# The last key chunk by paired block products inside the product with V, and the token maximum split over two batches

## The chip, the cores and the metric

The kernel runs on one core of one Trainium2 chip. A core has TensorE (PE in the profile; PEld are its weight loads), VectorE (DVE), ScalarE (ACT), GpSimd (POOL) and SyncE (SP, which here only issues DMAs). Matmul results go to PSUM, which has eight banks of 512 f32 columns; POOL works on SBUF only in this kernel. The metric is the device time of one execution in microseconds (us), given as a median of several runs.

## The reference, cut to what matters

There are 16 batches, each with 100 rows of x (640 wide), 718 rows of encoder states and 4 tokens (both 384 wide). All arithmetic is f32. Heads are 8 of 80 columns.

```python
query = hidden_states @ Wq                       # 100 x 640
keyt = enc @ Wk                                  # 718 x 640
valt = enc @ Wv                                  # 718 x 640
hs = _mha(query, keyt, valt)                     # 8 heads over 718 keys
ca_q1 = jnp.einsum('btc,th->bch', ca, Wq_ca)     # from the 4 tokens
ca_q1 = ca_q1[:, indices, :]                     # 100 of 384 rows
ca_hs1 = _mha(ca_q1, residual, residual)         # softmax 1, over the rows of x
ca_q2 = ca_hs1 @ Wq
ca_hs2 = _mha(ca_q2, ca @ Wk_ca, ca @ Wv_ca)     # softmax 2, over the 4 tokens
out = (hs + ca_hs2) @ Wout + b_out + residual
```

## The kernel before

The loop runs over the batches b. In batch b PE makes the scores and the values of b and, ahead of time, the keys of b + 1. The order of instructions on every engine is that of the program text, since the loop runs under a manual schedule; each engine works through its own list in order, and waits on semaphores where a tile that it reads or overwrites is not ready.

Keys and values are products of three row thirds and three column chunks of the encoder states with the weights. Most are not made by the usual 18 block products for a 3 x 3 by 3 x 2 block matrix but by 15, from sums of blocks (`V_PLAN` and `K_PLAN`). The sums of encoder blocks are made on POOL (`enc_sums`, L506), those of weights once at the start (`weight_sums`, L528). In a plan, each entry names a chain (A to E), a product and a place. The products of one chain are added up in one PSUM bank. After each product the bank, as it stands, is read once and goes to that entry's place: copied by ACT if the place is new (L413), added by DVE if it has been written before (L411). So the next product of a chain has to wait until the bank has been read.

The 640 key columns are five chunks of 128. Chunks 0 to 3 go through `Keys` (L471), two chunks a product. The fifth goes through `last_keys` (L565): nine plain matmuls of 128 columns of weights (`wk4`) with 240 keys, 18 passes since an f32 matmul makes two, into a pair of banks, and two copies by ACT (L576) into `kT`.

In a batch from the second to the one before the last, PE does in this order: scores in three groups (`s_ps`, L620), `z_ps` (L808) of the second softmax path, `y_ps` (L746), the transposes of the batch before (`hst_ps`), 15 value products and 15 key products in turns (L440, L471), `last_keys`, the projection of earlier rows (`o_ps`, L951, in 11 batches in all), the queries of the next two batches (`q_ps`, L541, in odd batches), and the product with V (`a_ps`, L1317). That has two groups of four heads; each entry of a group is a pair of matmuls, one with 64 columns of weights and one with 36, in the two column halves of PE's array, 81 columns wide. Group 0 goes first over the keys of all four heads by tile, group 1 head by head. After a group DVE takes the reciprocal of the sums (L1329), multiplies (L1331) and adds `hs2`, the token part (L1338).

The first softmax of the token path is over `e1` (100 x 800). POOL makes it for batch b + 1 (`scores1`, L781, L788) during batch b. Its maximum is found by `Maximum`: DVE turns the tile (L672), reduces it (L674, L677, L684), spreads the maxima (by DVE, L699, or, with `scalar`, by ACT, L694) and turns them back (L702); `softmax1` then subtracts (L798) and `exponentials1` takes the exponential on ACT (L801). In batches from the second on, all this stands after `last_keys` and ahead of `a_ps`. The keys' maxima of the main softmax (`most`, L1156 and L1168; `st`, L1144 and L1152) go through the same engines.

PSUM is in three pools of two: `ps2` (pairs of banks: block chains A and B of the values, `last_keys`, `o_ps`, scores groups 0 and 2), `psk` and `ps1` (single banks: the other chains, queries, scores group 1, `a_ps`). `psum` takes from the last two in turn. The row third (1, 0) and (2, 2) of the encoder states have a single tile, `rest`, which SP loads for batch b + 2 behind the reads of `last_keys` and of `enc_sums`.

Of the kernel before, what the change touches and what calls it, by code (L numbers as in the profile page):

```python
# [8 lines left out]
F32 = mybir.dt.float32  # L9
# [9 lines left out]
P = 128  # L19
# [56 lines left out]
def load_packed(load, to, w):  # L76
# [37 lines left out]
    ("A", 0, (0, 1)),  # L114
    ("B", 14, (0, 0)),
    ("A", 5, (1, 1)),
]

K_PLAN = [V_PLAN[k] for k in (0, 1, 2, 3, 4, 6, 5, 7, 9, 11, 8, 12, 10, 13, 14)]
# [13 lines left out]
def kernel(  # L133
# [117 lines left out]
    def a_form(enc, f):  # L251
        return enc[0][:, A_AT[f]]
# [4 lines left out]

    wv_sb = const.tile([P, NF, H // 2], F32, name="wv_sb")
    wk_sb = const.tile([P, NF, 2, P], F32, name="wk_sb")
    wk4 = const.tile([P, CC, P], F32, name="wk4")  # L260
    wq_sb = const.tile([P, HC, H], F32, name="wq_sb")
    kT = const.tile([P, HC, 3, KT], F32, name="kT")
    wout_sb = const.tile([P, HC, H], F32, name="wout_sb")
# [100 lines left out]
    e1 = const.tile([P, ROWS], F32, name="e1")  # L364
    nc.gpsimd.memset(e1[96:, :], LOW)

    ys = []
    for j in range(2):
        y = const.tile([S, NH, HT + 1], F32, name=f"y_{j}")
        nc.gpsimd.memset(y[:, :, HT:], 1.0)  # L370
        ys.append(y)


    def first_values(i, enc, engines, halves=(0, 1), get=psum):
# [19 lines left out]
    class Blocks:  # L394


        def __init__(self, plan):
            self.opened, self.begun = {}, set()
            self.plan = iter(enumerate(plan))
            self.ends = {bank: k for k, (bank, _, _) in enumerate(plan)}  # L400
# [15 lines left out]
    class Values(Blocks):  # L416
# [17 lines left out]
        def product(self, at, f, first, last):  # L434
            for bank in "AB":
                if self.opened[bank] is at and bank in self.fresh:
                    first = True
                    self.fresh.discard(bank)
            for j in range(2):
                nc.tensor.matmul(  # L440
                    at[0][j][:KN, : H // 2],
                    a_form(self.enc, f)[:, j * KN : (j + 1) * KN],
                    wv_there.get(f, wv_sb[:, W_AT[f]]),
                    start=first,
                    stop=last,
                    skip_group_check=True,
                )
# [142 lines left out]
    def last_keys(b, enc):  # L590
        banks = pair(f"kT_ps_{b}")
        return chunk_keys(
            HC - 1,
            [banks[:, k] for k in range(2)],
            [wk4[:, c] for c in range(CC)],
            enc,
        )


    def scores(b, g, tiles):  # L600
# [124 lines left out]
    class Second:  # L725


        def __init__(self, b, xT, ca=None):
            self.b, self.xT = b, xT[:, b % 2]
            self.top = None  # L730

            self.ca = ca
            if ca is not None:
                return
            self.ca = small.tile([S, T, S], F32, tag="ca", name=f"ca_{b}", bufs=2)
            nc.sync.dma_start(
                out=self.ca, in_=cas[b].unsqueeze(0).to_broadcast([S, T, S])
            )
# [23 lines left out]
            return summed  # L762

        def copy(self):
            b, y_ps = self.b, self.y_ps
            self.y = ys[b % 2]
            nc.scalar.copy(
                self.y[:, :, :HT].rearrange("p (u h) k -> p u h k", u=2),
                y_ps[:S, HT : 11 * HT].rearrange("p (u h k) -> p u h k", u=2, h=5)[
                    :, :, :4, :  # L770
                ],
            )
# [19 lines left out]
        def softmax1(self, n=8):  # L792

            if not self.top:
                self.top = Maximum(e1, f"1_{self.b}")
            self.top.go(n)
            if self.top.over is not None:
                nc.vector.tensor_tensor(e1[:S], e1[:S], self.top.over[:S], ALU.subtract)  # L798

        def exponentials1(self):  # L800
# [255 lines left out]
    for c in range(HC):  # L1056
        w_ps = psum(f"w_ps_{c}")
        for cc in range(CC):
            nc.tensor.transpose(
                w_ps[:, cc * P : (cc + 1) * P], wkt_sb[:, c, cc * P : (cc + 1) * P], ident  # L1060
            )
        act(
            wk_sb[:, c % 2 : 6 : 2, c // 2] if c < HC - 1 else wk4,
            w_ps[:, : CC * P].rearrange("p (a n) -> p a n", a=CC),
        )

# [55 lines left out]
    for b in range(B):  # L1122
# [38 lines left out]
        if b == 0:  # L1161
            enc_sums(enc)
            now.load()
            now.softmax1()
        st.append(scores(b, 0, tiles))
        if b == 0:
            now.exponentials1()
        nc.vector.tensor_tensor(most[:KN], st[0][:, 0], st[0][:, 1], ALU.max)  # L1168
        st.append(scores(b, 1, tiles))
# [12 lines left out]
        if b == 0:  # L1182
            second.scores1()
            m_next = load_m(b + 2)
            kk.go(3)
            top.go(3)
            first_values(3, e_in, (act, act), get=bank)
            top.go(1)
            kk.go(2)
            now.scores2()  # L1190
            first_values(0, e_in, (act, act), (0,), bank)
            top.go()
            kk.go(3)
            first_values(0, e_in, (act, act), (1,), bank)
            now.softmax3()
            kk.go(2)
            subtract(0)
            exponential(0)
            kk.go(2)
            subtract(1)  # L1200
            kk.go(3)
            exponential(1)
            second_next, enc_next = loads()
            less = subtract(2)
            exponential(2)
            last_keys(b + 1, enc)
            enc_next = load_rest(b + 2, enc_next)
            keys(m_next)
            now.values2(less)
            enc_sums(enc_next)  # L1210
            second.softmax1(4)
        elif b + 1 < B:
            if b > 1:
                last.transpose()
            vv = Values(b, e_in)

            def both(n):
                vv.go(n)
                kk.go(n)

            second.scores1(seen)
            if b == 1:
                now.load()
            last.load()
            top.go(3)
            both(3)
            now.scores2()
            top.go(1)
            both(2)
            if b == 1:  # L1230
                nc.vector.tensor_tensor(last.hs[:S], last.hs[:S], last.hs2, ALU.add)
            top.go()
            both(2)
            if b == 1:
                last.transpose(get=psum1)
            both(1)
            now.softmax3()
            now.values2()
            vv.go(2)
            kk.go(1)  # L1240
            subtract(0)
            exponential(0)
            vv.go(1)
            subtract(1)
            vv.go(1)
            kk.go(2)
            exponential(1)
            vv.go(1)
            kk.go(2)
            both(1)  # L1250
            both(1)
            if b == 1:
                for f in list(wv_there):
                    nc.scalar.copy(wv_sb[:, W_AT[f]], wv_there.pop(f))
            second.load()
            if b == 1:
                nc.gpsimd.dma_start(out=bias, in_=bout[0].partition_broadcast(P))
            second_next, enc_next = loads()
            if b + 2 < B:
                m_next = load_m(b + 2)  # L1260
            subtract(2)
            exponential(2)
            last_keys(b + 1, enc)
            if b + 2 < B:
                enc_next = load_rest(b + 2, enc_next)
            second.softmax1()
            last.project()
        else:
            room = enc_tile("spare").rearrange("p f k -> p (f k)")
            spare.extend(room[:, i * H : (i + 1) * H] for i in range(2))  # L1270
            last.transpose()
            vv = Values(b, e_in)
            last.load()
            mine.load()
            top.go(3)
            vv.go(3)
            last.project_few(len(OC) - 2)
            now.scores2()
            top.go(1)
            vv.go(2)  # L1280
            top.go()
            vv.go(3)
            now.softmax3()
            now.values2()
            vv.go(2)
            subtract(0)
            exponential(0)
            vv.go(5)
            for i in (1, 2):
                subtract(i)  # L1290
                exponential(i)
            last.project()
# [3 lines left out]
        if b % 2 and b + 1 < B:  # L1296
            xT, tiles = xT_at[0], queries_tiles(p + 1)
            for n in range(HC):
                queries(p + 1, xT, tiles, n)
        if 0 < b < B - 1:  # L1300
            second.exponentials1()

        mine.hs = hs = hs_tile(f"hs_{b}")
        hs2 = now.hs2
        for g in range(2):
# [3 lines left out]
            order = [(h, i) for h in range(4 * g, 4 * g + 4) for i in range(len(KC))]  # L1309
            if g == 0:  # L1310
                order.sort(key=lambda at: at[1] // 2)
            for h, i in order:
                if b == B - 1 and h == NH - 1 and i == 0:

                    mine.transpose([(0, 2)])
                for lo, hi in QC:
                    nc.tensor.matmul(  # L1317
                        a_v[lo:hi, h % 4],
                        st[i // 2][: KEYS[i], i % 2, h * S + lo : h * S + hi],
                        block(i, h // 4)[: KEYS[i], h % 4],  # L1320
                        start=(i == 0 and h in (0, *range(4, NH))),
                        stop=(i == len(KC) - 1),
                        skip_group_check=True,
                    )
# [71 lines left out]
```

## Time and profile before

| what | value |
| --- | --- |
| runs | 943.58, 943.99, 944.01 us; median 943.99 |
| span of the profiled execution, first to last instruction | 942.4 us; the page gives no other time of that execution |
| PE busy | 934.5 us, 99% of the span |
| DVE, POOL, ACT busy | 674.0, 623.1, 364.7 us |
| granted TensorE clock | 1.000 |
| chain that ended last: PE share | 96% |
| of it, `a_ps`; `kT_ps` | 12%; 8% |

A line of groups gives the source line, engine, operation, output and inputs, shape and count; then, after the bar, busy us in total and mean ns of one, and then the idle time of the engine just before, with what ended it. A timeline line gives start (us), duration (us), and the same names; an idle time is in square brackets. A line of waits has the waiting instruction, what it waited for, and the total us, the number and the longest. Durations of PE matmuls overlap, since they are pipelined; the chain of work in order of time gives each piece the time until the next one.

### The profile page before, as it was taken

The numbers are of one execution on the slowest core, as the hardware profiler recorded it, in microseconds if no ns is written. First come the engines' busy times: TensorE is split into PE (matmuls) and PEld (weight loads), VectorE is DVE, ScalarE is ACT, GpSimd is POOL, SyncE is SP. The second block draws the span as 40 slices with busy tenths as digits, with TensorE's granted clock in tenths as the row PEclk, the third lists the DMA queues.
The fourth block names the chain that finished last, engine by engine and source line by source line (L and its number), as shares of the span: only waits on it lengthen the run. The fifth ranks groups of instructions, "written<-read, shape, count | busy, mean of one in ns | idle before, by whom it ended". The sixth has DMA issues, their size and how long they took to land.

```text
span 942.4 us, 25629 instructions
## 1 busy us (share of the span) xinstructions
PE 934.5 (99%) x11215; PEld 796.2 (84%) x11215; DVE 674.0 (72%) x1084; ACT 364.7 (39%) x605; POOL 623.1 (66%) x565
## 2 busy tenths in 40 slices
PE   9999999999999999999999999999999999999998
PEld 6998979888797888989789887987989888897866
DVE  3559794977929688595955959578693886949684
ACT  1244443524334244433424334244431534334241
POOL 5857976776738757495873948657694576748514
PEclk9999999999999999999999999999999999999999
DMA  8822024040310404003050130403113030210300
GB/s 264 296 60 87 3 70 128 1 130 3 94 60 1 117 2 135 5 11 122 1 151 3 37 82 1 139 1 95 38 40 113 1 112 7 59 53 1 95 8 29
DMA packets 45367, 62.48 MB, mean 66 GB/s; under 512 B 13448, under 2 KB 37320, under 8 KB 43656
## 3 DMA queue, kind: packets, MB, share of 16 engines
q1 hardware_dynamic: 41720, 42.97, 15.2%
q0 software_dynamic: 2512, 16.72, 6.1%
q8 instruction: 88, 1.44, 0.6%
q10 hardware_dynamic: 1024, 1.15, 0.4%
q14 instruction: 23, 0.19, 0.1%
HBM read 55.26 MB, written 5.57 MB: 65 GB/s over the span
## 4 chain that ended last, share of the span: by engine, by line
PE 96%; DVE 3%; issue 0%; DMA 0%; ACT 0%; POOL 0%; ACTq 0%; DVEq 0%
PE s_ps L620 12%; PE a_ps L1317 12%; PE v_psA L440 10%; PE v_psB L440 8%; PE kT_ps L565 8%; PE k_psA L471 7%; PE q_ps L541 7%; PE o_ps L951 7%; PE k_psB L471 6%; PE v_psC L440 3%; PE k_psC L471 3%; PE y_ps L746 2%; PE v_ps L381 2%; PE v_psD L440 2%; PE v_psE L440 2%; PE k_psE L471 1%
## 5 line engine op out<-in xcount | busy, mean ns | idle before, releaser
L781 POOL TENSOR_TENSOR e<-ca,g 100x800 f32<-100x800 f32 x64 | 99.8, 1570 | 145.2 <-DVE most L1156 125.0
L870 POOL TENSOR_TENSOR hs<-vb,p 100x640 f32<-100x640 f32 x64 | 105.6, 1659 | 45.9 <-DVE p L856 32.5
L877 POOL TENSOR_TENSOR hs<-hs,hs 100x640 f32<-100x640 f32 x48 | 113.9, 2373 | 3.8
L1317 PEld LDWEIGHTS a_ps<-vs,st 120*36 120x36 f32 (+3 forms) x3072 | 109.1, 125 | 5.6 <-issue 5.5
L1317 PE MATMUL a_ps<-vs,st 120*36 120x81 f32 (+3 forms) x3072 | 111.9, 233 | 0.0
L440 PE MATMUL v_psA<-wv_sb,enc 128*120 128x320 f32 x352 | 109.5, 434 | 0.0
L506 POOL TENSOR_TENSOR enc<-enc 128x240 f32<-128x240 f32 x135 | 98.1, 736 | 16.9 <-DMA enc<-in_enct 9.8
L1144 DVE TENSOR_TENSOR st<-st,over 120x1600 f32<-120x1600 f32 x48 | 107.6, 2243 | 0.0
L637 ACT COPY st<-s_ps 120x800 f32<-120x800 f32 x64 | 49.7, 829 | 135.6 <-PE s_ps L620 135.6
L620 PE MATMUL s_ps<-qp,kT 32*120 32x100 f32 x3072 | 97.4, 263 | 0.0
L620 PEld LDWEIGHTS s_ps<-qp,kT 32*120 32x120 f32 x3072 | 94.7, 179 | 1.6 <-issue 0.2
L788 POOL TENSOR_TENSOR e<-e,e 100x800 f32<-100x800 f32 x48 | 90.4, 1884 | 3.8
L440 PE MATMUL v_psB<-wv_sb,enc 128*120 128x320 f32 x296 | 91.9, 433 | 0.0
L471 PE MATMUL k_psA<-enc,wk_sb 128*128 128x240 f32 x360 | 87.6, 366 | 0.0
L1329 DVE RECIPROCAL rs<-a_ps 100x4 f32<-100x4 f32 x32 | 5.8, 182 | 111.0 <-PE a_ps L1317 111.0
L1156 DVE TENSOR_TENSOR most<-most,st 120x800 f32<-120x800 f32 x64 | 66.2, 1034 | 24.1 <-ACT st L631 23.0
L1152 ACT ACTIVATE st<-st 120x1600 f32<-120x1600 f32 x48 | 73.9, 1539 | 22.3 <-DVE st L1144 22.2
L471 PEld LDWEIGHTS k_psA<-enc,wk_sb 128*128 128x128 f32 x360 | 68.2, 190 | 16.8 <-DVE kT L411 0.2
L440 PEld LDWEIGHTS v_psA<-wv_sb,enc 128*120 128x120 f32 x352 | 63.2, 183 | 22.6 <-issue 0.5
L471 PE MATMUL k_psB<-enc,wk_sb 128*128 128x240 f32 x300 | 73.1, 366 | 0.3 <-DVE sm L853 0.3
L440 PEld LDWEIGHTS v_psB<-wv_sb,enc 128*120 128x120 f32 x296 | 54.0, 183 | 21.9 <-DVE vs L411 0.4
L541 PE MATMUL q_ps<-xT,wq_sb 128*128 128x200 f32 x400 | 69.1, 333 | 0.0
(146 smaller groups left out, 1732.8 us busy)
## 6 DMA issues: line engine op xcount, KB each, us to landing
vb<-va_d POOLq DMA_DIRECT2D x16, 1000.0 KB, 7.4
enc<-in_enct SPq DMA_DIRECT2D x30, 240.0 KB, 3.9
enc<-in_enct SPq DMA_DIRECT2D x15, 360.0 KB, 3.6
xT<-in_xt SPq DMA_DIRECT2D x8, 500.0 KB, 4.3
rest<-in_enct SPq DMA_DIRECT2D x31, 120.0 KB, 6.6
xn<-in_x SPq DMA_DIRECT2D x11, 320.0 KB, 5.7
out<-xn SPq DMA_DIRECT2D x11, 320.0 KB, 3.2
ca<-in_cas SPq DMA_DIRECT2D x16, 156.2 KB
```

What stands on the lines that cost most here:

```text
L440: nc.tensor.matmul(at[0][j][:KN, : H // 2], a_form(self.enc, f)[:, j * KN : (j + 1) * KN], wv_there.get(f, wv_sb[:, W_AT[f]]), start=first ...
L471: nc.tensor.matmul(at[:, i * KT : (i + 1) * KT], wk_sb[:, W_AT[f], i], a_form(self.enc, f), start=(first and i == 0), stop=last, skip_grou ...
L506: nc.gpsimd.tensor_tensor(out, left, right, op)
L541: nc.tensor.matmul(q_ps[:, : 2 * S].rearrange("p (j s) -> p j s", j=2), wq_sb[:, c, n * P : (n + 1) * P], xT[:, :, c, :], start=(c == 0), ...
L565: nc.tensor.matmul(bank[:, i * KT : (i + 1) * KT], weights[c], a_raw(enc, u, c), start=(i == 0 and c == 0), stop=(c == CC - 1), skip_group ...
L620: nc.tensor.matmul(s_ps[r][:n, 256 * a + lo : 256 * a + hi], kT[rows, c, u, j * KN : (j + 1) * KN], rhs, start=(a == 0 and c == 0), stop=( ...
L781: first = nc.gpsimd.tensor_tensor(to, self.ca[:, t, :].unsqueeze(1).to_broadcast([S, NH, S]), g[:, :, t].unsqueeze(2).to_broadcast([S, NH, ...
L788: nc.gpsimd.tensor_tensor(e, e, to, ALU.add)
L870: first = nc.gpsimd.tensor_tensor(to, vb[:S, t, :].rearrange("p (h d) -> p h d", h=NH), p2[:, :, t].unsqueeze(2).to_broadcast([S, NH, D]), ...
L877: nc.gpsimd.tensor_tensor(sums, sums, to, ALU.add)
L1144: return nc.vector.tensor_tensor(st[i], st[i], top.over[:KN].unsqueeze(1).to_broadcast([KN, 2, ROWS]), ALU.subtract,)
L1317: nc.tensor.matmul(a_v[lo:hi, h % 4], st[i // 2][: KEYS[i], i % 2, h * S + lo : h * S + hi], block(i, h // 4)[: KEYS[i], h % 4], start=(i ...
```

## The change

The fifth chunk of the keys of batches 2 to 15 is no longer made by `last_keys`. It is made by the same 15 block products, with `wk5` holding 64-column blocks of weights and their sums (the differences are made once, on POOL, in batch 1). `REST_PLAN` puts them in eight steps. Seven steps are two products of 64 columns of weights with 240 keys, one in each column half of PE's array, in two banks; one step is a single product, split in its keys over the halves. The steps stand inside the product with V: one after the first pair of each group of heads, and then every six pairs, four steps in each group. After a step its two partial sums are read from PSUM, by ACT where the place in `kT` is new and by DVE where it has been written. Chain A has six of the products, in steps 0, 2, 4, 5, 6 and 7. Banks A and B are from `psk`, D and C are a pair of `ps2`. The first two key sets (batches 0 and 1) still go through `last_keys`.

The maximum of `e1` for batches from 2 on is spread by ACT instead of DVE, and stops there ahead of the projection; the transpose back and the subtraction go to the start of the next batch, ahead of its scores, and the exponential behind the copies of its first scores. One `y` tile is left of two.

```diff
@@ -114,6 +114,17 @@
     ("A", 0, (0, 1)),
     ("B", 14, (0, 0)),
     ("A", 5, (1, 1)),
+]
+
+REST_PLAN = [
+    (("A", 7, (2, 1)), ("B", 13, (1, 0))),
+    (("D", 1, (2, 0)), ("C", 12, (0, 1))),
+    (("A", 3, (2, 0)), ("B", 8, (2, 0))),
+    (("E", 6, (1, 0)),),
+    (("A", 9, (1, 0)), ("C", 11, (2, 1))),
+    (("A", 2, (0, 0)), ("B", 10, (2, 1))),
+    (("A", 0, (0, 1)), ("B", 4, (0, 1))),
+    (("A", 5, (1, 1)), ("B", 14, (0, 0))),
 ]
 
 K_PLAN = [V_PLAN[k] for k in (0, 1, 2, 3, 4, 6, 5, 7, 9, 11, 8, 12, 10, 13, 14)]
@@ -257,7 +268,7 @@
 
     wv_sb = const.tile([P, NF, H // 2], F32, name="wv_sb")
     wk_sb = const.tile([P, NF, 2, P], F32, name="wk_sb")
-    wk4 = const.tile([P, CC, P], F32, name="wk4")
+    wk5 = const.tile([P, NF, P // 2], F32, name="wk5")
     wq_sb = const.tile([P, HC, H], F32, name="wq_sb")
     kT = const.tile([P, HC, 3, KT], F32, name="kT")
     wout_sb = const.tile([P, HC, H], F32, name="wout_sb")
@@ -364,11 +375,8 @@
     e1 = const.tile([P, ROWS], F32, name="e1")
     nc.gpsimd.memset(e1[96:, :], LOW)
 
-    ys = []
-    for j in range(2):
-        y = const.tile([S, NH, HT + 1], F32, name=f"y_{j}")
-        nc.gpsimd.memset(y[:, :, HT:], 1.0)
-        ys.append(y)
+    y_sb = const.tile([S, NH, HT + 1], F32, name="y_sb")
+    nc.gpsimd.memset(y_sb[:, :, HT:], 1.0)
 
 
     def first_values(i, enc, engines, halves=(0, 1), get=psum):
@@ -592,9 +600,69 @@
         return chunk_keys(
             HC - 1,
             [banks[:, k] for k in range(2)],
-            [wk4[:, c] for c in range(CC)],
+            [
+                wk5[:, 2 * c : 2 * c + 2].rearrange("p g n -> p (g n)")
+                for c in range(CC)
+            ],
             enc,
         )
+
+    class LastKeys:
+
+
+        def __init__(self, b, enc):
+            self.b, self.enc = b, enc
+            self.banks, self.begun = {}, set()
+            self.steps = iter(REST_PLAN)
+
+        def product(self, bank, half, f, lo, keys, n, first):
+            nc.tensor.matmul(
+                bank[64 * half : 64 * half + 64, lo : lo + n],
+                wk5[:, W_AT[f]],
+                a_form(self.enc, f)[:, keys : keys + n],
+                start=first,
+                stop=True,
+                skip_group_check=True,
+            )
+
+        def read(self, bank, half, to, lo, keys, n):
+            u, g = to
+            out = kT[64 * g : 64 * g + 64, HC - 1, u, keys : keys + n]
+            left = bank[64 * half : 64 * half + 64, lo : lo + n]
+            if to in self.begun:
+                nc.vector.tensor_tensor(out, left, out, ALU.add)
+            else:
+                nc.scalar.copy(out, left)
+
+        def open(self, chains):
+            name = f"k5_ps_{self.b}"
+            if chains == "AB":
+                self.banks |= {c: psumk(f"{name}_{c}") for c in "AB"}
+            elif chains == "DC":
+                both = pair(name)
+                self.banks |= {"D": both[:, 0], "C": both[:, 1]}
+
+        def go(self, n=1):
+            for _, step in zip(range(n), self.steps):
+                if len(step) == 1:
+                    ((_, f, to),) = step
+                    parts = [
+                        (self.banks[c], half, f, to, KT, half * KN, KN, False)
+                        for half, c in enumerate("DC")
+                    ]
+                else:
+                    first = step[0][0] not in self.banks
+                    if first:
+                        self.open("".join(c for c, _, _ in step))
+                    parts = [
+                        (self.banks[c], half, f, to, 0, 0, KT, first)
+                        for half, (c, f, to) in enumerate(step)
+                    ]
+                for bank, half, f, _, lo, keys, m, first in parts:
+                    self.product(bank, half, f, lo, keys, m, first)
+                for bank, half, _, to, lo, keys, m, _ in parts:
+                    self.read(bank, half, to, lo, keys, m)
+                self.begun |= {to for _, _, to in step}
 
 
     def scores(b, g, tiles):
@@ -727,7 +795,7 @@
 
         def __init__(self, b, xT, ca=None):
             self.b, self.xT = b, xT[:, b % 2]
-            self.top = None
+            self.top, self.less = None, False
 
             self.ca = ca
             if ca is not None:
@@ -762,8 +830,8 @@
             return summed
 
         def copy(self):
-            b, y_ps = self.b, self.y_ps
-            self.y = ys[b % 2]
+            y_ps = self.y_ps
+            self.y = y_sb
             nc.scalar.copy(
                 self.y[:, :, :HT].rearrange("p (u h) k -> p u h k", u=2),
                 y_ps[:S, HT : 11 * HT].rearrange("p (u h k) -> p u h k", u=2, h=5)[
@@ -792,9 +860,10 @@
         def softmax1(self, n=8):
 
             if not self.top:
-                self.top = Maximum(e1, f"1_{self.b}")
+                self.top = Maximum(e1, f"1_{self.b}", self.b > 1)
             self.top.go(n)
-            if self.top.over is not None:
+            if self.top.over is not None and not self.less:
+                self.less = True
                 nc.vector.tensor_tensor(e1[:S], e1[:S], self.top.over[:S], ALU.subtract)
 
         def exponentials1(self):
@@ -1060,7 +1129,9 @@
                 w_ps[:, cc * P : (cc + 1) * P], wkt_sb[:, c, cc * P : (cc + 1) * P], ident
             )
         act(
-            wk_sb[:, c % 2 : 6 : 2, c // 2] if c < HC - 1 else wk4,
+            wk_sb[:, c % 2 : 6 : 2, c // 2]
+            if c < HC - 1
+            else wk5[:, :6].rearrange("p (a g) n -> p a (g n)", a=CC),
             w_ps[:, : CC * P].rearrange("p (a n) -> p a n", a=CC),
         )
 
@@ -1161,9 +1232,9 @@
         if b == 0:
             enc_sums(enc)
             now.load()
-            now.softmax1()
+        now.softmax1()
         st.append(scores(b, 0, tiles))
-        if b == 0:
+        if b != 1:
             now.exponentials1()
         nc.vector.tensor_tensor(most[:KN], st[0][:, 0], st[0][:, 1], ALU.max)
         st.append(scores(b, 1, tiles))
@@ -1254,16 +1325,16 @@
                     nc.scalar.copy(wv_sb[:, W_AT[f]], wv_there.pop(f))
             second.load()
             if b == 1:
+                weight_sums(nc.gpsimd, wk5)
                 nc.gpsimd.dma_start(out=bias, in_=bout[0].partition_broadcast(P))
             second_next, enc_next = loads()
             if b + 2 < B:
                 m_next = load_m(b + 2)
             subtract(2)
             exponential(2)
-            last_keys(b + 1, enc)
             if b + 2 < B:
                 enc_next = load_rest(b + 2, enc_next)
-            second.softmax1()
+            second.softmax1(4)
             last.project()
         else:
             room = enc_tile("spare").rearrange("p f k -> p (f k)")
@@ -1297,8 +1368,7 @@
             xT, tiles = xT_at[0], queries_tiles(p + 1)
             for n in range(HC):
                 queries(p + 1, xT, tiles, n)
-        if 0 < b < B - 1:
-            second.exponentials1()
+        k5 = LastKeys(b + 1, enc) if 0 < b < B - 1 else None
 
         mine.hs = hs = hs_tile(f"hs_{b}")
         hs2 = now.hs2
@@ -1309,7 +1379,9 @@
             order = [(h, i) for h in range(4 * g, 4 * g + 4) for i in range(len(KC))]
             if g == 0:
                 order.sort(key=lambda at: at[1] // 2)
-            for h, i in order:
+            for at, (h, i) in enumerate(order):
+                if k5 and at % 6 == 1:
+                    k5.go()
                 if b == B - 1 and h == NH - 1 and i == 0:
 
                     mine.transpose([(0, 2)])
```

## The prediction

> **What bounds the kernel now.** I read the page's busy times first, then the chain of work that ended last, then the waits of TensorE.
>
> ```profile
> PE 934.5 (99%) x11215; PEld 796.2 (84%) x11215; DVE 674.0 (72%) x1084; ACT 364.7 (39%) x605; POOL 623.1 (66%) x565
> PE 96%; DVE 3%; issue 0%; DMA 0%; ACT 0%; POOL 0%; ACTq 0%; DVEq 0%
> ```
>
> TensorE (PE) is busy for 99% of the span at the full granted clock, and the chain is PE. The chain in order of time (start, us, what, passes; each f32 matmul makes two passes) shows two batches:
>
> ```profile
> 49.44 1.77 PE va_ps L1090 x12
> ...
> 365.52 3.65 PE kT_ps L565 x18
> 369.17 8.46 PE q_ps L541 x50
> 377.62 6.91 PE a_ps L1317 x191
> 384.53 7.28 PE s_ps L620 x240
> ...
> 422.39 3.65 PE kT_ps L565 x18
> 426.04 5.38 PE o_ps L951 x20
> 431.42 6.91 PE a_ps L1317 x191
> ```
>
> Each piece starts where the last one ended, so a batch has no slack: a us taken from PE is a us gained, and a us that PE waits is a us lost. The waits of PE confirm it; the longest, in the whole run, is
>
> ```profile
> PE k_psE L471 <- DVE vs L411: 1.2, 1, 1.2
> ```
>
> **What is removed.** The 18-pass product kT_ps (3.65 us, 0.203 us a pass of 240 columns) goes in batches 1 to 14: 14 x 3.65 = 51.1 us.
>
> **What is added on PE.** Eight steps, placed among the 48 pairs of a_ps (6.91/48 = 0.144 us a pair): after one pair, and then every six pairs, 6 x 0.144 = 0.864 us. Seven steps are a pair of 240-column products in the two column halves, one a pair of 120. Do halves overlap? a_ps is such a pair already, and va_ps is the nearest in width: 6 pairs of passes of 320 columns in 1.77 us with start and drain, 0.295 at most each. Scaled to 240 that is 0.221; if only the columns count, 0.203. A step thus costs 0.406 to 0.442, all eight 3.04 to 3.32. I take the lower end, since the start and drain are paid once: 14 x (3.65 - 3.04) = 8.5 us gained (4.6 at the other end).
>
> The Trainium skill, "TensorE: Matmul & The Clock Gate", Part 3, The mechanism, says that weight loads overlap running matmuls only when their row groups differ. Column halves share all rows, so by it the four loads of a pair would be bare; at the page's columns/1.2 ns (Part 2) that is 53 ns each, an estimate of 0.21 us a step and 22 us in all, and the sum below would end at +34. The va_ps row is against it.
>
> **What is added as waits.** Before, kT_ps was copied once into kT, and PE waited for nothing. Now chain A adds six products into one bank, and each product waits until the partial sum before it was read. Two of these reads are late, by the order of instructions on VectorE (DVE).
>
> Step 5 (the second of head group 1) waits for DVE's add of step 4 in bank A. On DVE that add stands behind the reciprocal, multiply and hs2 add of head group 0:
>
> ```profile
> 381.21 0.18 DVE L1329 RECIPROCAL rs<-a_ps 100x4 f32<-100x4 f32 x1 [7.34 <-PE a_ps L1317]
> 381.43 0.49 DVE L1331 TENSOR_TENSOR hs<-a_ps,rs 100x320 f32<-100x320 f32 x1
> 382.03 0.95 DVE L1338 TENSOR_TENSOR hs<-hs,hs 100x320 f32<-100x320 f32 x1
> ```
>
> Here the last add ran beside GpSimd (POOL) sums; beside an idle POOL, in batch 7:
>
> ```profile
> 498.09 0.49 DVE L1338 TENSOR_TENSOR hs<-hs,hs 100x320 f32<-100x320 f32 x1
> ```
>
> Count from the reciprocal's start. Group 1 began 0.20 before (half of 6.91 after 377.55 is 381.01). Step 5 is due one pair, one step and six pairs later: 0.144 + 0.406 + 0.864 - 0.20 = 1.21. The hs2 add starts at 0.82 and takes 0.49 alone, 0.60 to 1.03 beside POOL (mean of the eight such rows 0.83). The new 64x240 add is sized from the DVE groups that read PSUM:
>
> ```profile
> L411 DVE TENSOR_TENSOR kT<-k_psA,kT 128x480 f32<-128x480 f32 x45 | 29.2, 648 | 0.2
> L411 DVE TENSOR_TENSOR vs<-v_psC,vs 120x320 f32<-120x320 f32 x30 | 14.5, 490 | 7.8 <-PE v_psC L440 7.2
> L576 ACT COPY kT<-kT_ps 128x240 f32<-128x240 f32 x20 | 7.3, 363 | 2.6 <-PE kT_ps L565 2.6
> ```
>
> One ns a column: 0.41 at 240. Back-to-back DVE instructions overlap by 0.07. What it costs PE to start again is seen in batch 0:
>
> ```profile
> 85.44 0.64 DVE L411 TENSOR_TENSOR kT<-k_psC,kT 128x480 f32<-128x480 f32 x1
> ...
> 86.13 1.08 PE L471 MATMUL k_psC<-enc,wk_sb 128*128 128x240 f32 x4 [0.33 <-DVE kT L411]
> ```
>
> From 86.08 to 86.13 is 0.05, and the first pass with its weight load bare takes 0.1 more: 0.15. So step 5 starts at 0.82 + 0.83 - 0.07 + 0.41 + 0.15 = 2.14 beside POOL, 1.80 alone: 0.93 or 0.59 late. POOL is in its enc sums at that moment in batches 1, 2, 4, 5, 6, 8, 9, 10, 12 and 13, idle in 3, 7, 11, taken as idle in 14: 10 x 0.93 + 4 x 0.59 = 11.7 us. Bounds: all alone with a restart of 0.05, 14 x 0.49 = 6.9; all at 1.03, 14 x 1.13 = 15.8.
>
> Step 7 waits for both adds of step 6, which go to the same rows of kT, so one follows the other. A DVE add starts 0.22 after PE's slot ends (rs: 0.20): 0.22 + 0.41 + 0.41 + 0.15 = 1.19 against 0.864: 0.33 late, 14 x 0.33 = 4.6. Bounds: 1.5 (overlap of 0.07 and a restart of 0.05 make it 0.11) to 5.6. The other steps make it: the adds of step 3 (0.29 each at 120 columns) end 0.73 after its slot, due 0.864; the ScalarE (ACT) copies (0.363) have a full period more.
>
> Batches 1, 5, 9 and 13 have queries and no projection, and there bank B of step 0 is the one that the last query chunk left. It is free when ACT's two qz copies end (0.11 + 0.74 after the queries; 377.66, 0.74 in the timeline of ACT). Half B starts at 0.85 + 0.13 = 0.98 instead of 0.09 + 0.14: 0.75, 4 x 0.75 = 3.0 (2.4 to 4). Also there, the queries now start 3.65 earlier while ACT first spreads the token maximum (2 x 0.849) once DVE has reduced it; the fifth chunk waits for the first copy: 0.2, in batch 1 0.5, together 1.1 (0 to 2).
>
> **What costs nothing, and under what cover.** The token maximum's transpose and subtraction (1.01 + 0.99 on DVE) move to the start of the next batch. DVE finishes hs 1.3 to 1.8 after a_ps, so these end by 3.8, and the first maximum of the scores starts 4.3 after a_ps (388.77 against 384.46); a late end would only hold the exponential (0.87 on ACT), due before z_ps at 7.3, with four score copies behind it 0.1 later. The two ACT spreads in place of DVE's two reductions and copy lie beside PE. One y tile instead of two: the ACT copy waits for z_ps, which PE has issued before y_ps. The twelve wk5 differences (12 x 0.34 = 4.0 on POOL, once, in batch 1) delay step 0 to 148.4, where the wait for qz has it anyway; the m2 products and enc sums queued behind them are needed 15 us later. On SP's queue the two loads of rest stay in place but no longer wait for kT_ps; POOL's 39.1 us of waits for them shrink, which keeps POOL busy at the hs2 add in all ten batches, already priced. SP's later stores and xn loads only move earlier. kT's last chunk is read 1.5 us after step 7, its add ends at 0.63.
>
> **Sum.** -8.5 + 11.7 + 4.6 + 3.0 + 1.1 = +11.9 us. The profiled span is 942.4; the median of the runs, 943.99, is 1.6 above it. 943.99 + 11.9 = 955.9. Best ends of the waits: -8.5 + 6.9 + 1.5 + 2.4 + 0 = +2.3, 946.3. Worst: -4.6 + 15.8 + 5.6 + 4 + 2 = +22.8, 966.8.
>
> **Rivals.**
> Faster: the one read that decides is step 4's add. If it is done within 0.864 of its step, as every other read is (almost), nothing waits and 8.5 us stay: 935.5. For it: the block products of this same kernel read and add in the same manner with PE never waiting after batch 0. Against: they have 2 us between uses of a bank, and here 1.7 us of DVE work stands ahead. It decides against my sign once the wait per batch falls under 0.6. Chance 0.12.
> About equal: step 5 waits at its lower bound, the others hardly; the waits (8.5) eat the gain: 944. Chance 0.08.
> The halves overlap for one pass of two only, since a product's two passes follow each other and an isolated pair has nothing to fill in: 3 passes a pair, 0.2 x 7.5 x 14 = 21 us more, 977. Against it, va_ps and a_ps. Chance 0.05.
>
> **How the numbers follow.** The forecast has 0.75: 955.9, its own range 946 to 967. What a measurement tells from no change is about 0.2%, 1.9 us. Faster is 0.12 (the first rival), same 0.08, slower 0.80. The range leaves out the faster rival and the serial one (0.17) and takes in the equal one: 943 to 967.
>
> **What the profile after would show.** Right: PE idle named by the 64x240 add on DVE in every batch, 0.5 to 1 us in step 5; a smaller one in step 7; PE waiting for ACT's qz in four batches; no kT_ps after batch 0; the eight steps 0.4 us each where nothing waits. Wrong: a stretch of a_ps with its steps under 10.3 us and no PE idle (the first rival), or steps of 0.6 us and more without an idle gap (halves in series). My sum falls if the hs2 add is shorter than its rows, or if PE goes on with the a_ps pairs behind a waiting product.

## The result and the profile after

The changed kernel takes 955.55 us (median of 4 runs, 953.81 to 956.51) against 944.0 before: a ratio of 1.012, 95% interval 1.0106 to 1.0134. It is slower, by about what was forecast (955.9). The profiled span is 954.2, 11.8 above the 942.4 of before.

The page after, busy times and the chain of work that ended last:

```profile
PE 940.7 (99%) x11411; PEld 788.2 (83%) x11411; DVE 706.6 (74%) x1182; ACT 404.6 (42%) x689; POOL 620.0 (65%) x576
PE 89%; DVE 4%; POOL 3%; DMA 1%; issue 1%; ACT 0%; SPq 0%; DVEq 0%; POOLq 0%
```

PE's share of the chain fell from 96 to 89%, which is some 67 us and so no measure of the 11.6 lost: most of GpSimd's 3% is one stretch from 114.5 to 147.9 us, along which the chain is followed back from step 0 of batch 1, where the wait itself is at most 0.4 us (for the `wk5` differences, below). PE still reads as 99% busy: its idle time is 13.5 us, only 5.6 more than before, since the records of neighbouring matmuls overlap and cover part of a hole. The chain in order of time shows it; this is batch 4, from the first pair of the product with V to the scores (start, us, what):

```profile
320.20 0.28 PE a_ps L1389 x3
320.48 0.19 PE k_ps_B L619
320.69 0.18 PE k_ps_B L619
320.89 0.84 PE a_ps L1389 x24
321.74 0.41 PE k_ps L619 x4
...
325.44 0.50 DVE hs L1403
...
326.04 0.67 DVE hs L1410
326.70 0.32 DVE kT L633
327.03 0.04 issue
327.07 0.42 PE k_ps_A L619
...
331.28 7.28 PE s_ps L688 x240
```

A step is 0.41 us and six pairs are 0.84, so nothing waits until step 4. Then the chain leaves PE for VectorE's reciprocal, multiply (L1403), hs2 add (L1410) and the add of step 4 (L633), and step 5 starts where that add ends. The waits of PE and of its weight loads say the same; four of the rows that the new steps brought are

```profile
PE k_ps_A L619 <- DVE kT L633: 5.7, 14, 0.8
PEld k_ps_B L619 <- DVE kT L633: 2.4, 13, 0.2
PEld k_ps_B L619 <- ACT qz L561: 1.7, 3, 0.6
PEld k_ps_B L619 <- POOL wk L536: 0.4, 1, 0.4
```

These are 14 waits of chain A (step 5, one a batch), 13 of bank B (step 7), 3 for qz (step 0 of batches 5, 9 and 13) and, at step 0 of batch 1, one for the `wk5` differences that GpSimd makes there. The time from the first pass of step 4 to that of step 5, read from the starts of the matmuls, is 1.74 to 2.32 us; between the other full steps it is 1.25 to 1.30 in the ten batches without queries. From step 7 to the scores it is 1.58.

### The profile page after: what moved, and what is told of

It reads as the page before. It is cut to its first block, busy times and chain, and to the rows that moved or that the text cites. A ratio compares the mean times of both kernels' runs of the same rounds, so it can differ in the third digit from the quotient of the medians.

```text
span 954.2 us, 26279 instructions
## 1 busy us (share of the span) xinstructions
PE 940.7 (99%) x11411; PEld 788.2 (83%) x11411; DVE 706.6 (74%) x1182; ACT 404.6 (42%) x689; POOL 620.0 (65%) x576
## 4 chain that ended last, share of the span: by engine, by line
PE 89%; DVE 4%; POOL 3%; DMA 1%; issue 1%; ACT 0%; SPq 0%; DVEq 0%; POOLq 0%
PE s_ps L688 12%; PE a_ps L1389 10%; PE v_psA L448 10%; PE v_psB L448 8%; PE k_psA L479 7%; PE q_ps L549 6%; PE o_ps L1020 6%; PE k_psB L479 6%; PE v_psC L448 3%; PE k_psC L479 2%; PE k_ps_A L619 2%; PE kT_ps L573 2%; PE y_ps L814 2%; PE v_psD L448 2%; PE v_ps L389 2%; PE v_psE L448 2%
## 5 line engine op out<-in xcount | busy, mean ns | idle before, releaser
L1389 PEld LDWEIGHTS a_ps<-vs,st 120*64 120x64 f32 (+3 forms) x3072 | 133.0, 124 | 14.2 <-issue 5.5
L1389 PE MATMUL a_ps<-vs,st 120*64 120x81 f32 (+3 forms) x3072 | 142.6, 234 | 0.0
L633 DVE TENSOR_TENSOR kT<-k_ps_A,kT 64x240 f32<-64x240 f32 x42 | 16.7, 397 | 92.3 <-PE k_ps_A L619 81.8
```

Of the source, the lines that this page charges most:

```text
L1389: nc.tensor.matmul(a_v[lo:hi, h % 4], st[i // 2][: KEYS[i], i % 2, h * S + lo : h * S + hi], block(i, h // 4)[: KEYS[i], h % 4], start=(i ...
```

## The experiments

Each kernel stood beside the kernel before on its own chip (944.28 and 944.16 us in the two groups).

**The hs2 add of group 0 behind step 5.**

```diff
                 if k5 and at % 6 == 1:
                     k5.go()
+                if k5 and g == 1 and at == 7:
+                    nc.vector.tensor_tensor(
+                        hs[:S, add_later], hs[:S, add_later], hs2[:, add_later], ALU.add
+                    )
...
-            if b:
+            if k5 and g == 0:
+                add_later = cols
+            elif b:
                 nc.vector.tensor_tensor(hs[:S, cols], hs[:S, cols], hs2[:, cols], ALU.add)
```

> The hs2 add of head group 0 is put behind step 5 on VectorE instead of ahead of the adds of step 4; nothing else moves. Theory (step 5 waits for the add in bank A, which stands behind reciprocal, multiply and hs2 add): that add then ends 0.71 - 0.05 + 0.41 = 1.07 us after the reciprocal's start, and with a restart of 0.15 step 5 could begin at 1.22, due at 1.21. The interval from step 4 to step 5, 1.74 to 2.32 in the trace after (27.9 in sum over 14 batches), falls to the 1.25 of the others; 955.55 - 10.3 - 0.7 for the restarts = 944.5. Rival (the interval is long because step 4 is the first of a new head group, a new bank and weights, or because product C of step 4 waits for the adds of step 3): the interval stays and so does the time, 955.5. Step 7 still waits in both.

947.06 us, ratio 1.0028 (1.0018 to 1.0038): 8.5 us of the 11.6 are gone. VectorE in batch 4 of this kernel:

```profile
322.73 0.49 DVE L1407 TENSOR_TENSOR hs<-a_ps,rs 100x320 f32<-100x320 f32 x1
323.14 0.39 DVE L633 TENSOR_TENSOR kT<-k_ps_A,kT 64x240 f32<-64x240 f32 x1
323.56 0.41 DVE L633 TENSOR_TENSOR kT<-k_ps,kT 64x240 f32<-64x240 f32 x1
324.40 0.41 DVE L633 TENSOR_TENSOR kT<-k_ps_B,kT 64x240 f32<-64x240 f32 x1 [0.44 <-PE k_ps_B L619]
324.85 0.83 DVE L1386 TENSOR_TENSOR hs<-hs,hs 100x320 f32<-100x320 f32 x1
325.70 0.40 DVE L633 TENSOR_TENSOR kT<-k_ps_A,kT 64x240 f32<-64x240 f32 x1
```

The add of step 4 (323.14) now follows the multiply, ends at 323.53, and step 5 begins on time: the interval is 1.25 in ten batches, and 1.34 to 1.45 in the four with queries. The bank, the new head group and the weights are the same as before, so the rival falls. 2.5 us of the expected gain are missing, because the wait moved a little: the hs2 add beside GpSimd (0.83 above) now ends as the adds of step 6 are due, and in batches 4, 6, 10 and 12 the time from step 6 to the scores is 0.05 to 0.3 us longer than it was, in batch 14 almost 1.0. So the move alone is still slower than the kernel before, by 2.8 us.

**Step 7 two pairs later.**

```diff
-                if k5 and at % 6 == 1:
+                if k5 and at in ((1, 7, 13, 19), (1, 7, 13, 21))[g]:
```

> Step 7 alone is put two pairs later (0.28 us) in the second head group. Theory (its half B waits 0.33 us for the second add of step 6, which runs behind the first on VectorE): the halves of step 7 start together, the time from step 7 to the scores falls by the two pairs and by the wait of 0.28, and 14 x 0.28 = 3.9 us go: 951.6. Rival (the long end of the product with V is the change of tile form before the scores, or a wait for the last chunk of the keys): nothing goes, or the scores wait for the later key add, 955.5 or more.

951.82 us, 3.7 below the changed kernel as a difference of medians, as expected. In the chain of this kernel, step 7 of batch 4 and the scores:

```profile
327.99 1.12 PE a_ps L1389 x32
329.12 0.20 PE k_ps_A L619
329.32 0.09 PE k_ps_B L619
329.41 0.11 PE k_ps_A L619
329.52 0.07 PE k_ps_B L619
329.59 0.45 PE a_ps L1389 x11
330.04 1.98 PE s_ps L688 x61
```

The halves start within 0.1 us of each other, and step 7 to scores takes 1.02 us in nearly all batches, 0.56 less than before for 0.28 of pairs moved. The scores don't wait for the key add that now comes later.

**The queries' banks the other way round in batches 1, 5, 9 and 13.**

```diff
             xT, tiles = xT_at[0], queries_tiles(p + 1)
+            turn[0] += 1 - turn[0] % 2
             for n in range(HC):
```

> In batches 1, 5, 9 and 13 the queries take their banks in the other order, so that the fifth chunk's bank is no longer bank B of step 0. Theory: the 0.54 to 0.6 us that step 0 loses there to the two qz copies go, 4 x 0.55 = 2.2 us: 953.3. Rival (step 0 is late there for another reason, the spread of the token maximum on ScalarE being the candidate): no change, 955.5.

953.61 us, 1.9 below. In batch 5 step 0 starts without a wait, both halves at once; here PE's timeline:

```profile
377.91 0.35 PE L1390 MATMUL a_ps<-vs,st 120*64 120x81 f32 x4
378.09 0.37 PE L619 MATMUL k_ps_B<-enc,wk 128*64 128x240 f32 x1
378.11 0.37 PE L619 MATMUL k_ps_A<-enc,wk 128*64 128x240 f32 x1
```

In the changed kernel half A's two passes started at 377.97 and 378.18 there, half B's first only at 378.69. The gain is near the bound of what this comparison can tell, but the row of waits for qz is gone. Batch 1 gains little: half B still waits for the `wk5` differences there, and step 1 comes 0.15 us earlier instead of the 0.56 of the three others.

**All three together.**

> All three moves together. Theory: the gains add, 955.55 - 11.0 - 3.9 - 2.2 = 938.5, under the kernel before by 5.5 us, near the 935.5 to 936 of a change that makes no wait. Rival (the waits only move: with PE earlier, another read becomes the late one, the second add of step 6 at step 7 or the add of step 5 at step 6): less than the sum, 941 to 946.

941.3 us, ratio 0.9968 (0.9956 to 0.9979): faster than the kernel before, less so than the sum, at the rival's lower edge. The waits left are the moved ones: step 7 to scores is 1.03 where the hs2 add ran alone and 1.23 to 1.32 in six batches where it ran beside GpSimd, and batch 14 loses 0.84 at step 7 and behind it.

**The add behind step 7, and the spread between query copies.** On top of the second and third move, instead of the first:

```diff
-            second.softmax1(4)
+            second.softmax1(3 if b % 2 else 4)
...
                 queries(p + 1, xT, tiles, n)
+                if n == 1 and b > 0:
+                    second.softmax1(1)
...
-            if b:
+            if k5 and g == 0:
+                add_later = cols
+            elif b:
+                if k5:
+                    nc.vector.tensor_tensor(
+                        hs[:S, add_later], hs[:S, add_later], hs2[:, add_later], ALU.add
+                    )
                 nc.vector.tensor_tensor(hs[:S, cols], hs[:S, cols], hs2[:, cols], ALU.add)
```

> As the kernel with all three moves, but the hs2 add of group 0 stands behind step 7 (with that of group 1), and in odd batches ScalarE spreads the token maximum between the second and third query copy instead of ahead of all. Theory: in the trace of the three moves the end of the product with V is 1.03 us where the add ran beside an idle GpSimd and 1.24 to 1.49 where not, and step 7 starts 0.37 late in batch 14; with the add behind step 7 it is 1.03 everywhere, 6 x 0.25 + 0.84 + 0.2 = 2.5 us; the waits of the fifth query chunk (0.8 in three batches) go as well: 941.3 - 3.3 = 938.0. Rival: VectorE's longer tail (0.5 to 1.0 us) at the start of the next batch makes the token softmax late and TensorE waits at z_ps: 941 or more.

938.74 us, ratio 0.9939 (0.9926 to 0.9951), 5.4 us under the kernel before. Its product with V with the steps takes 10.09 or 10.10 us in batches 2 to 14, without exception, and PE's longest wait is again the one that the kernel before had:

```profile
PE k_psE L479 <- DVE vs L419: 1.2, 1, 1.2
```

At z_ps the weight loads wait 3.9 us in all, as in the kernel before, so VectorE's longer tail is covered. The two moves were not run apart; by the traces the product with V became 2.3 us shorter in sum over the batches, and the queries of batches 5, 9 and 13 0.24 each.

**The token part alone**, on the kernel before:

```diff
-                self.top = Maximum(e1, f"1_{self.b}")
+                self.top = Maximum(e1, f"1_{self.b}", self.b > 1)
...
-            now.softmax1()
+        now.softmax1()
         st.append(scores(b, 0, tiles))
-        if b == 0:
+        if b != 1:
             now.exponentials1()
...
-            second.softmax1()
+            second.softmax1(4)
...
-        if 0 < b < B - 1:
-            second.exponentials1()
```

> The kernel before with only the token part of the change: the maximum stops ahead of the projection, ScalarE spreads it, transpose, subtraction and exponential go to the next batch. Theory: no product of TensorE moves and nothing of it is waited for, so the time is that of the kernel before, 944.0 within 0.2%. Rival (part of the 11.6 us is the token part, its transpose and subtraction at the start of a batch holding up the score maxima): 946 or more.

944.39 us, ratio 1.0004 (0.9995 to 1.0013): no change, as expected of work beside PE.

**The keys alone**, with the token softmax whole ahead of the product with V (the same lines the other way, in the changed kernel).

> The changed kernel with the token softmax left whole ahead of the product with V, as before. Theory: ScalarE's copies of step 0 and 1 then stand behind the exponential, which ended 9.5 us after the start of kT_ps in the trace before (431.72 against 422.23); in the seven even batches step 2 is due at 8.2 and waits for a copy that ends at 9.9: 1.8 x 7 = 13 us more, 967. Rival (the token part gives the steps nothing): 955.5.

972.9 us, ratio 1.0302 (1.0288 to 1.0316). The token part is worth 17 us once the steps are there. ScalarE in batch 4:

```profile
325.30 0.87 ACT L870 ACTIVATE e<-e 100x800 f32<-100x800 f32 x1 [5.62 <-DVE e L867]
326.19 0.35 ACT L635 COPY kT<-k_ps_A 64x240 f32<-64x240 f32 x1
```

and PE's longest waits:

```profile
PE k_ps_A L619 <- ACT kT L635: 11.2, 7, 1.6
PE k_ps_A L619 <- DVE kT L633: 6.9, 14, 0.9
```

The copy of step 0 stands behind an exponential that waits for VectorE, and chain A with it: from step 1 to step 2 it is 2.99 to 3.08 us in the even batches instead of 1.26, 12.4 in sum, as priced. The other 5 of the 17 were not priced: step 3 follows 0.2 later in the same batches (the halves no longer in step), step 0 of batch 1 waits for the wk5 differences on GpSimd (0.9), and the interval before step 5 is over 1.75 in eleven batches instead of eight, 2.7 us in sum.

**The steps without the reads.** This kernel makes the products but nothing reads their sums:

```diff
-                for bank, half, _, to, lo, keys, m, _ in parts:
-                    self.read(bank, half, to, lo, keys, m)
```

> The changed kernel with the eight steps' products, but nothing reads their partial sums, so the last key chunk of batches 2 to 15 is not made (this is what it leaves out). Theory: the pairs run in both halves at once at 0.41 us a step and only the reads made PE wait; the steps cost 14 x 3.1 us against 51.1 removed, and the qz and query waits of four batches (3.0) stay: 944.0 - 7.5 + 3.0 = 939.5. Rival (the added time is the products themselves, halves one after the other): 955 or more.

940.59 us, ratio 0.9959 (0.9943 to 0.9974): 15 us of the changed kernel's time are the reads. In the chain, batch 4, around step 5 in group 1:

```profile
323.71 0.85 PE a_ps L1387 x24
324.55 0.18 PE k_ps_B L619
324.74 0.02 PE k_ps_A L619
324.76 0.18 PE k_ps_B L619
324.94 0.02 PE k_ps_A L619
324.96 0.85 PE a_ps L1387 x24
```

Both halves finish two passes in 0.41 us, with six pairs before and after. The product with V takes 9.98 us with the steps in the ten batches without the qz wait, against 6.91 before: the steps cost 3.07 a batch. The time is 1.1 above the expected, since what stays in the four query batches is 4.5 us by this trace and not 3.0: 3.1 from the late halves of step 0 and 1.4 in the queries (9.23 and three times 8.79 against 8.55).

## Why the prediction was right

Term by term, the predicted us beside the measured ones (from the starts of PE's matmuls in the trace after, against those of the kernel without reads):

| term | predicted | measured | how |
| --- | --- | --- | --- |
| products, 14 x (3.65 - steps) | -8.5 | -8.1 | the eight steps of a batch 3.07, taken as 3.04 |
| step 5 | +11.7 | +11.0 | sum of intervals 27.9 - 14 x 1.255 = 10.3, first pass slower by 0.05 x 14 |
| step 7 | +4.6 | +4.3 | 0.36 in ten batches (1.58 - 1.22), 0.15 to 0.21 in four |
| qz, four batches | +3.0 | +3.1 | 10.74 - 9.98 in three for qz, 0.83 in batch 1 for the `wk5` differences |
| fifth query chunk | +1.1 | +1.2 | start of q_ps to a_ps 8.97, 8.80, 8.79, 8.80 against 8.55 |
| sum | +11.9 | +11.5 | span +11.8, medians +11.55 |

What carried the forecast: PE had no slack, so the sign hung on the waits alone; and the order of VectorE's list, not its 74% of busy time, said which read would be late. Against the measured terms the moved add took away 8.5 of 11.0 us, and its trace has about 1.6 of the rest again behind step 6; the later step 7 took 3.7 of 4.3, the swapped banks 1.9 of 3.1 (batch 1 has another cause), and the missing reads 15.0 of the 15.3 of steps 5 and 7. So these causes are shown. The first rival needed the add of step 4 within 0.864 us of its step; in batch 6, one of six where the hs2 add took its shortest time, it ended 1.28 us after:

```profile
437.87 0.18 DVE L1401 RECIPROCAL rs<-a_ps 100x4 f32<-100x4 f32 x1
438.09 0.49 DVE L1403 TENSOR_TENSOR hs<-a_ps,rs 100x320 f32<-100x320 f32 x1
438.68 0.49 DVE L1410 TENSOR_TENSOR hs<-hs,hs 100x320 f32<-100x320 f32 x1
439.09 0.39 DVE L633 TENSOR_TENSOR kT<-k_ps_A,kT 64x240 f32<-64x240 f32 x1
```

Halves in series are refuted by the steps of 0.41 us. The Trainium skill, "TensorE: Matmul & The Clock Gate", Part 3, The mechanism, says that weight loads overlap running matmuls only when the row groups differ; with four bare loads at the price of Part 2 a step would take about 0.62 us, an estimate that the same 0.41 refutes.

Smaller misses inside the right sum. The hs2 add was taken as slowed in ten batches, at 0.83; it was slowed in eight (0.58 to 1.02, mean 0.80) and took 0.49 in batches 6 and 12, although the loads of rest did come sooner (GpSimd's waits for them fell from 39.1 us to 6.3). A restart was taken at 0.15 from a row with 128 columns of weights; with 64 it is 0.05 to the weight load and 0.05 in the first pass (0.25 after a wait against 0.20). The two errors are of the same sign: with the measured adds and a restart of 0.10 the prediction's own sum for step 5 is 10.1 instead of 11.7. It was luck that 0.9 us came back from a cause that it did not have: in the ten other batches the interval from step 4 to step 5 is 1.25 or 1.26 plus the hs2 add, in the four query batches 1.46 to 1.55 plus the add, because the halves come there already 0.2 apart (last section). So the 0.4 us between forecast and median flatter it; the lower bound for step 7 was also added up wrong (0.22 + 0.41 + 0.41 + 0.05 - 0.07 is 0.16 above 0.864, not 0.11), which would put the best end at 947.0. That the token part costs nothing held; that it was needed by the steps' copies on ScalarE was not said, and the kernel with the keys alone showed it to be worth 17 us.

## What to carry to other kernels

Where an accumulator is read after every product, the time between two products of one chain has to hold the drain of the pipe, the read, a restart (here 0.2 to 0.3, 0.4 and 0.1 us), and whatever stands ahead of the read in its engine's list: find that list's longest neighbour, and put it where no product waits behind it. One add of 0.5 to 1.0 us, moved by a few places, took back 8.5 of the 11.6 us that the change lost; only with the other two moves did it gain (3.0 us against the kernel before on the same chip), and with the add at the very end and the spread of the maximum between the queries it gained 5.4. A part that does nothing for the time alone (the token part) can be what makes another part bearable, so parts are to be tried alone and together.

## What was not expected of the hardware

Once only one half of a pair has waited, the halves stay apart. In batch 5 after, half B of step 0 starts 0.7 us behind half A; from then on a step's first and last pass start 0.43 apart instead of 0.22, until the wait at step 5 holds both. The period of the steps stays 1.25, but without reads, where nothing brings the halves together again, the way from step 7 to the scores is 1.43 us in these batches against 1.22. One late half is paid twice: with the wait (0.57 at step 0), and with 0.2 where the halves have to meet.

How long the hs2 add takes depends on how much of GpSimd's running sum is left when it starts, and not only on whether GpSimd is at work. Batch 4, GpSimd's lines and VectorE's together:

```profile
324.89 1.47 POOL L514 TENSOR_TENSOR enc<-enc 128x240 f32<-128x240 f32 x2
326.04 0.67 DVE L1410 TENSOR_TENSOR hs<-hs,hs 100x320 f32<-100x320 f32 x1
326.31 0.94 POOL L514 TENSOR_TENSOR enc<-enc,rest 128x240 f32<-128x240 f32 x1
```

The sum that runs when the add starts ends at 326.36, the add 0.35 later. The sum that starts during the add takes 0.94 instead of 0.70 and ends 0.55 after it. In batch 6 the add took 0.49 us, although GpSimd ran sums on either side of its start:

```profile
438.03 0.69 POOL L514 TENSOR_TENSOR enc<-rest,enc 128x240 f32<-128x240 f32 x1
438.80 1.70 POOL L514 TENSOR_TENSOR enc<-enc 128x240 f32<-128x240 f32 x2
```

The add began at 438.68, when the first of them had 0.04 left, and the next two sums took 1.70 instead of the 1.36 of the two before. The whole trace after keeps to this: each of the ten hs2 adds of 0.58 us or more, of both head groups, ends 0.35 us after the sum that ran at its start, and each of the nine GpSimd sums that start during an hs2 add ends 0.55 or 0.56 after the add. So the two take turns here, and whichever starts first goes ahead; no run varied it on purpose. The 0.83 us of the prediction was thus a mean over chance positions, and the sum of the intervals before step 5 shifts with them: 27.9 us in the changed kernel, 27.5 with step 7 later, 28.1 with the banks swapped.
